# Layer 1 of a four-layer transformer kernel: feature maps of the attention moved to VectorE, its column of ones kept, one scaling moved ahead, separate PSUM banks for the last experts of layer 0, two TensorE fillers

## Chip, core and metric

The kernel runs on one core of a Trainium2 chip. The metric is the device time of one execution in microseconds (us). The engines named below are TensorE (PE, with its weight loads as PEld), VectorE (DVE), ScalarE (ACT), GpSimd (POOL) and SyncE (SP), which issues DMAs.

## What is computed

Four layers act on a residual x of 8 x 512 tokens of width 128, all in float32. Each layer is x = x + attention(layernorm(x)), then x = x + ffn(layernorm(x)). Layer 0 ends with a mixture of 16 small experts per head. The change lies mainly in the attention of layer 1, a linear attention with 16 heads of width 8:

```
def _feature_map(t): return jax.nn.elu(t) + 1.0
q, k, v = split(x @ w_qkv.T);  q, k = _feature_map(q), _feature_map(k)
kv = einsum('bhnd,bhne->bhde', k, v)
out = einsum('bhnd,bhde->bhne', q, kv) / (einsum('bhnd,bhd->bhn', q, k.sum(axis=2))[..., None] + 1e-06)
return out @ w_out.T
```

The feature map is elu(t) + 1, which is exp(t) for t below 0 and t + 1 above. It can be written min(exp(t), 1) + max(t, 0), and also exp(min(t, 0)) + max(t, 0). The FFN of layer 1 is a gated product over all tokens (called z in the code), and for 256 chosen tokens a choice of one of 8 experts. Layers 2 and 3 follow, with the experts of layer 2 and the linear layers of layer 3.

## The kernel before

The tokens are handled in eight blocks b of 512, each as J = 4 tiles of 128. Every engine executes its instructions in the order in which the program issues them: the order is written by hand, and so a step that waits holds up all that is behind it on its engine.

**Layer 0, the experts** (from L659). The units are (b, e), eight blocks by sixteen experts. `first_half` (L549) makes four products into PSUM and applies Gelu on ScalarE into `hm`; of its four results one goes to the bank `p1` and three to one of two triple banks, `threes[e % 2]`. `second_half` (L566) multiplies `hm` by the second weights into one bank from `bank()`, VectorE multiplies by the gate (L575), and POOL adds to `acc` (L581); for the very last unit the product is kept apart and not added. The loop at L681 issues the first half of unit n and the second half of unit n - 2, so for the last two turns (n = 128 and 129) only second halves are left. In this stage the pool has a single bank "one" (L533), and `bank()` (L185) gives that one unless `banks["own"]` is set. In the middle of a turn `side("P", n)` may take one step of side work on PE. `finish` (L583) multiplies the accumulated block by the output weights and adds to the residual (L270).

**Layer 1, the loop.** The tuple `stages` (L1179) lists the steps of one turn, each with a lag; at L1219 the turn i issues each step f for block i + lag. The steps that matter here:
- `turn_` (L753): four PE transposes of the normalised block `xn`, then a ScalarE copy to `xt` (L750).
- `scale`: four ScalarE instructions (L726) that make `xn` of the next block. Tiles 0 to 2 are issued after `turn_`, tile 3 as the last step of the turn.
- `project_q` (L819): q = weights x `xt` into one bank, then `exponential` (L811): Exp (L814) and Relu (L815), both from PSUM into SBUF. `q_map` (L824): POOL takes min(exp, 1) (L827) and adds relu (L828).
- `project_kv` (L830): eight products into a pair of banks, `exponential` of the keys, then a ScalarE copy of the values to `v` (L837), a tile of 129 columns. `k_map` (L839): VectorE makes the keys from exp and relu (L842), and POOL sets the 129th column of `v` to one (L843), which gives the sum of the keys.
- `gather` (L845): products of k and v on PE, then three VectorE steps to `kv`. `attend` (L861): products of q and `kv`, then VectorE divides. `turn_o` (L884): transposes and a ScalarE copy to `ot` (L889). `output` (L891): the output product and VectorE's addition to the residual (L270).
- the FFN steps `f_stats`, `f_scale`, `f_turn`, `f_gate`, `z_stats`, `z_scale`, `z_turn`, `z_out`, with lags of -3 to -7, so that only the last turns have all of them.

PSUM has two pairs "two" and four single banks "one" here (L2136), given out in turn.

**After the loop** (L1224 on) the rest is issued by hand. The normalised rows of the chosen tokens are written to DRAM by `f_scale` (DMAs at L905) and fetched by two indirect DMAs in `chosen_rows` (L999). `chosen_products` (L1006) transposes the rows and makes the gate and expert products; `chosen_gates`, `chosen_select` (L1069, L1070 on VectorE, L1073 on POOL) and others follow. At the end the first block is normalised for layer 2, POOL scatters the chosen outputs (L1169) and makes the last additions (L988, L1301), and the first queries of layer 2 follow on PE (`queries`, L1450), which need `qb`, a VectorE instruction (L2103).

`keep_clock(n)` (L777) issues n products of the identity with itself into a bank that nobody reads. It exists and is called in layers 0 and 3.

Of the kernel before, what the change touches and what calls it, by code (L numbers as in the profile page):

```python
# [160 lines left out]
def body(ctx, tc, dram, spans, x_in, ib, it, ic, ei, out):  # L161
# [114 lines left out]
    def layer0():  # L276
# [7 lines left out]
        with ExitStack() as st:  # L284
# [351 lines left out]
            with tc.manual_schedule():  # L636
# [32 lines left out]
                def first(n):  # L669
                    if n < len(units):  # L670
                        hms[n] = first_half(*units[n])
# [8 lines left out]

                for n in range(len(units) + 2):  # L681
                    first(n)

                    banks["own"] = threes[(n + 1) % 2][:, 0, :]
                    b, e = units[min(n, len(units) - 1)]
                    if e == 4 and b > 0:
                        finish(b - 1)
                    else:
                        side("P", n)
                    banks.pop("own")  # L690
                    second(n)
# [48 lines left out]
    def scale(b, part=(0, J)):  # L740
        if part[0] == 0:
            t[b]["xn"] = norm.tile([P, J, D], F32, tag="xn", name="xn")
        scaled(t[b]["xn"], x[b], t[b]["by"], part[1], part[0])
# [50 lines left out]
    def layer1():  # L794
# [9 lines left out]
        with tc.tile_pool(name="l1", bufs=2) as wp, tc.tile_pool(name="l1c", bufs=1) as once:  # L804
# [3 lines left out]
            top_row = once.tile([P, P], F32, tag="top_row", name="top_row")  # L808
            ebs = once.tile([P, 2, TB], F32, tag="ebs", name="ebs")

            def exponential(tag, src, shape):  # L811
                ex = wp.tile(shape, F32, tag=f"ex{tag}", name="ex")
                re = wp.tile(shape, F32, tag=f"re{tag}", name="re")
                nc.scalar.activation(ex, src, AF.Exp)  # L814
                nc.scalar.activation(re, src, AF.Relu)  # L815
                return ex, re


            def project_q(b):  # L819
                pq = bank()  # L820
# [1 line left out]
                t[b]["eq"] = exponential("q", pq, [P, TB])  # L822

            def q_map(b):  # L824
                ex, re = t[b]["eq"]
                t[b]["q"] = wp.tile([P, TB], F32, tag="q", name="q")
                nc.gpsimd.tensor_scalar(ex, ex, 1.0, None, ALU.min)  # L827
                nc.gpsimd.tensor_tensor(t[b]["q"], ex, re, ALU.add)  # L828

            def project_kv(b):  # L830
                pk = bank2()
                pkv = pk.rearrange("p a (j n) -> p (a j) n", j=2)
                for j in range(J):
                    mm(pkv[:, j, :], cols(t[b]["xt"], j), l1["wqkv"][:, P:])
                t[b]["ek"] = exponential("k", pkv[:, :, :P], [P, J, P])
                t[b]["v"] = v = wp.tile([P, J, P + 1], F32, tag="v", name="v")
                nc.scalar.copy(v[:, :, :P], pkv[:, :, P:])  # L837

            def k_map(b):  # L839
                ex, re = t[b]["ek"]  # L840
                t[b]["k"] = wp.tile([P, J, P], F32, tag="k", name="k")
                nc.vector.scalar_tensor_tensor(t[b]["k"], ex, 1.0, re, ALU.min, ALU.add)  # L842
                nc.gpsimd.memset(t[b]["v"][:, :, P : P + 1], 1.0)  # L843

            def gather(b):  # L845
                ps = bank()
# [329 lines left out]
            def chosen_put():  # L1176
# [14 lines left out]
                (z_turn, -7),  # L1191
                (output, -2),
                (k_map, 0),
                (f_gate, -6),
                (turn_o, -1),
                (z_out, -7),
                (f_turn, -3),
                (z_stats, -6),
                (lambda b: scale(b, (3, J)), 1),
            )  # L1200
            with tc.manual_schedule():

                nc.scalar.activation(
                    stat.tile([P, J], F32, tag="nb", name="nb")[:, :1], half[:, :1], AF.Exp
                )
                for zt in zts:
                    nc.gpsimd.memset(zt[64:65, :], 1.0)
                nc.gpsimd.memset(top_row, 0.0)
# [41 lines left out]
                z_turn(2)  # L1250
                f_gate(4)
                z_stats(4)
                chosen_products()
                chosen_gates()
                z_scale(3)
# [34 lines left out]
                by = stats_of(x[0], J)  # L1290
                z_turn(6)
                z_scale_by_vector(7)
                z_out(5)
                z_turn(7, True)
                xn = norm.tile([P, J, D], F32, tag="xn", name="xn")
# [873 lines left out]
```

## Time and profile before

| what | us |
|---|---|
| median of 3 runs | 1468.98 (1465.3 to 1469.53) |
| profiled execution, time | 1466.0 |
| profiled execution, span | 1464.2 |
| PE busy | 1387.7 (95%) |
| ACT, DVE, POOL busy | 1042.7, 982.4, 647.3 |
| layer 1 in the trace | about 396 to 523 |

The span is what the trace covers; the time of that execution is 1.8 us more. All positions below are microseconds from the start of the span. A group line gives line, engine, operation, tiles, shapes and count, then total busy time and the mean of one in ns, then the idle time of the engine ahead of it and what ended it. A timeline line gives start and length, both in us. PEclk is the granted clock of TensorE, 1.00 being full.

### The profile page before, as it was taken

To read this page: it belongs to the slowest core of one execution; us is meant where nothing else is said; L and a number is where in the kernel's file an instruction comes from. 1 tells how busy PE (TensorE), PEld (TensorE's weight loads), DVE (VectorE), ACT (ScalarE), POOL (GpSimd) and SP (SyncE) were. 2 spreads that over 40 slices of the span, in tenths; PEclk is the share of its full clock that TensorE was granted. 3 is DMA by queue.
4 is the path that set the end of the run, shared out by engine and by line. 5 is a ranking of instruction groups with operands and counts; after the bars stand their busy time and mean duration, and the time that the engine had idled before them with its cause. 6 is when DMAs were issued, how large, how long until landed. Compare 5 with 4: busy or idle time off the path is not lost.

```text
span 1464.2 us, 22177 instructions
## 1 busy us (share of the span) xinstructions
PE 1387.7 (95%) x7708; PEld 665.4 (45%) x7708; DVE 982.4 (67%) x2061; ACT 1042.7 (71%) x2131; POOL 647.3 (44%) x746
## 2 busy tenths in 40 slices
PE   7789999999889899999999999999999999999996
PEld 3652222222267554444443444455454454554465
DVE  6776655676367667633672586786787777877876
ACT  6869999999867556664865486876876767768632
POOL 6646666665655433211620172442532623524423
PEclk9999999999999999999999999999999999999999
DMA  5039999998340010101000000000000000000000
GB/s 172 1 47 133 133 132 127 131 130 123 90 150 23 26 42 22 37 1 29 1 1 1 1 1 8 1 1 8 1 1 8 1 8 1 1 8 1 1 8 15
DMA packets 33232, 59.42 MB, mean 41 GB/s; under 512 B 5601, under 2 KB 25633, under 8 KB 28642
## 3 DMA queue, kind: packets, MB, share of 16 engines
q1 hardware_dynamic: 32416, 56.18, 22.1%
q10 hardware_dynamic: 578, 1.57, 0.3%
q8 instruction: 61, 1.00, 0.3%
q14 instruction: 49, 0.40, 0.1%
q0 software_dynamic: 128, 0.26, 0.1%
HBM read 49.70 MB, written 8.29 MB: 40 GB/s over the span
## 4 chain that ended last, share of the span: by engine, by line
PE 68%; ACT 13%; DVE 9%; DMA 6%; issue 2%; POOL 1%; SPq 0%; POOLq 0%; DVEq 0%; ACTq 0%
PE ps L246 66%; DMA gs<-gates 5%; ACT hm L563 5%; ACT ex L1486 2%; ACT hm L562 2%; DVE nm L1480 1%; DVE s L715 1%; DMA gates<-eq 1%; ACT xn L1402 1%; PE ps L1816 1%; DVE x L270 1%; ACT xn L726 1%; POOL rs L243 0%; ACT h L384 0%; SPq L543 0%
## 5 line engine op out<-in xcount | busy, mean ns | idle before, releaser
L1486 ACT ACTIVATE ex<-ps,nm 128x512 f32<-128x512 f32 x512 | 346.1, 688 | 182.7 <-DVE nm L1480 178.3
L1480 DVE TENSOR_REDUCE nm<-ps 128x2 f32<-128x1024 f32 x256 | 300.4, 1215 | 60.9 <-PE ps L246 60.3
L246 PE MATMUL ps<-q,k 64*128 64x512 f32 x1024 | 256.7, 617 | 5.6 <-ACT ex L1486 4.7
L246 PE MATMUL ps<-ex,vs 128*64 128x512 f32 x1024 | 233.8, 598 | 0.0
L581 POOL TENSOR_TENSOR acc<-acc,pr 128x512 f32<-128x512 f32 x119 | 166.5, 1399 | 108.2 <-DVE pr L575 100.8
L1501 POOL TENSOR_TENSOR vs<-v,sm 128x256 f32<-128x256 f32 x128 | 81.4, 636 | 295.0 <-DVE sm L1500 267.7
L563 ACT ACTIVATE hm<-ps,blob_f 128x1536 f32<-128x1536 f32 x128 | 196.3, 1534 | 0.0
L246 PE MATMUL ps<-xt,blob_a 128*128 128x512 f32 x304 | 152.4, 628 | 0.0
L575 DVE SCALAR_TENSOR_TENSOR pr<-ps,blob_f,gs 128x512 f32<-128x512 f32 x120 | 90.0, 750 | 90.1 <-PE ps L246 73.3
L246 PE MATMUL ps<-h,w 32*128 32x512 f32 x1024 | 148.0, 639 | 2.3 <-ACT xt L750 0.8
L246 PEld LDWEIGHTS ps<-q,k 64*128 64x128 f32 x1024 | 87.1, 185 | 136.7 <-issue 69.9
L246 PE MATMUL ps<-hm,w 128*32 128x512 f32 x1024 | 136.4, 605 | 4.3 <-DVE pr L575 3.8
L246 PEld LDWEIGHTS ps<-ex,vs 128*64 128x64 f32 x1024 | 67.8, 136 | 148.5 <-issue 130.8
L1688 POOL TENSOR_TENSOR acs<-acs,prod 128x512 f32<-128x512 f32 x98 | 124.7, 1273 | 11.0 <-ACT prod L1687 6.6
L242 POOL TENSOR_SCALAR rs<-mv 128x4 f32<-128x4 f32 (+1 forms) x69 | 18.0, 261 | 198.2 <-DVE mv L1392 140.7
L1486 ACT ACTIVATION_READ_ACCUMULATOR ex<-ps,nm 128x1 f32 x512 | 104.9, 205 | 0.0
L562 ACT ACTIVATE hm<-ps,blob_f 128x512 f32<-128x512 f32 x128 | 88.1, 688 | 17.9 <-PE ps L246 17.7
L246 PEld LDWEIGHTS ps<-xt,blob_a 128*128 128x128 f32 x304 | 53.2, 194 | 87.6 <-issue 61.2
L246 PEld LDWEIGHTS ps<-h,w 32*128 32x128 f32 x1024 | 40.9, 183 | 110.3 <-ACT hm L562 92.8
L1448 DVE TENSOR_TENSOR v<-ps,blob_bc 128x512 f32<-128x512 f32 x64 | 44.2, 691 | 67.5 <-PE ps L246 43.0
L246 PEld LDWEIGHTS ps<-blob_a,ct 128*128 128x128 f32 x512 | 67.0, 191 | 32.3 <-issue 29.2
L243 POOL TENSOR_TENSOR rs<-rs,half 128x4 f32<-128x4 f32 (+1 forms) x69 | 72.5, 1051 | 5.8
(303 smaller groups left out, 2183.9 us busy)
## 6 DMA issues: line engine op xcount, KB each, us to landing
gs<-gates SPq DMA_DIRECT2D x256, 128.0 KB
blob_f<-in_f SPq DMA_DIRECT2D x1, 2560.0 KB
blob_a<-in_a SPq DMA_DIRECT2D x1, 2056.0 KB
x<-in_x SPq DMA_DIRECT2D x8, 256.0 KB
gates<-eq SPq DMA_DIRECT2D x8, 256.0 KB
ge<-gates SPq DMA_DIRECT2D x4, 512.0 KB
back<-nought SPq DMA_DIRECT2D x7, 256.0 KB
by_rows<-fxn SPq DMA_DIRECT2D x7, 256.0 KB
```

The lines of the kernel that those rows point to most:

```text
L242: nc.gpsimd.tensor_scalar(t, var, EPS, None, ALU.add)
L243: nc.gpsimd.tensor_tensor(t, t, half[:, : t.shape[-1]], ALU.pow)
L246: nc.tensor.matmul(out_, lhs, rhs, start=start, stop=stop)
L562: nc.scalar.activation(hm[:, 0, :], p1, AF.Gelu, bias=bias)
L563: nc.scalar.activation(hm[:, 1:, :], p3, AF.Gelu, bias=bias)
L575: nc.vector.scalar_tensor_tensor(pr, po, f0["b2"][:, e : e + 1], gs, ALU.add, ALU.mult)
L581: nc.gpsimd.tensor_tensor(acc[:, b, :], acc[:, b, :], pr, ALU.add)
L1448: nc.vector.tensor_tensor(v, pv, bias, ALU.add)
L1480: nc.vector.tensor_reduce(nm, ps, AX.X, ALU.max, negate=True)
L1486: nc.scalar.activation(ex[kt][:, i, :], ps[:, i, :], AF.Exp, bias=nm[:, i : i + 1], accum_out=sm[:, kt, i : i + 1],)
L1501: nc.gpsimd.tensor_tensor(vs[:, tiles, :, :], vs_[n][:, tiles, :].rearrange("p j (i n) -> p j i n", i=2), sm[:, tiles, :].unsqueeze(3).to_ ...
L1688: nc.gpsimd.tensor_tensor(t["acs"], t["acs"], p, ALU.add)
```

## The change

- In layer 0, for the last two turns of the loop, the second half writes to the second and the third bank of `threes[0]`, and the step of side work is left out of these turns.
- `exponential` computes relu(-t) from PSUM, then exp of its negative in place, which is exp(min(t, 0)); it hands on the PSUM source beside it.
- Both maps are one VectorE instruction, max(t, 0) + that, with t read from PSUM. POOL's two instructions of the query map are gone.
- `v` is one of two lasting tiles, whose columns of ones are set once, ahead of the loop; the POOL instruction in `k_map` is gone.
- Tile 3 of the next block's scaling is issued right after `k_map`, ahead of `f_gate`, `turn_o` and what follows.
- `keep_clock(9)` is put ahead of `chosen_products`, and `keep_clock(6)` ahead of `z_out(5)`.

```diff
                 for n in range(len(units) + 2):
                     first(n)
+                    if n >= len(units):
+
+                        banks["own"] = threes[0][:, 1 + n - len(units), :]
+                        second(n)
+                        banks.pop("own")
+                        continue
...
+            vts = [once.tile([P, J, P + 1], F32, tag=f"v{i}", name="v") for i in range(2)]
...
             def exponential(tag, src, shape):
                 ex = wp.tile(shape, F32, tag=f"ex{tag}", name="ex")
-                re = wp.tile(shape, F32, tag=f"re{tag}", name="re")
-                nc.scalar.activation(ex, src, AF.Exp)
-                nc.scalar.activation(re, src, AF.Relu)
-                return ex, re
+                nc.scalar.activation(ex, src, AF.Relu, scale=-1.0)
+                nc.scalar.activation(ex, ex, AF.Exp, scale=-1.0)
+                return src, ex
+
+            def feature_map(dst, src, ex):
+                nc.vector.scalar_tensor_tensor(dst, src, 0.0, ex, ALU.max, ALU.add)
...
             def q_map(b):
-                ex, re = t[b]["eq"]
                 t[b]["q"] = wp.tile([P, TB], F32, tag="q", name="q")
-                nc.gpsimd.tensor_scalar(ex, ex, 1.0, None, ALU.min)
-                nc.gpsimd.tensor_tensor(t[b]["q"], ex, re, ALU.add)
+                feature_map(t[b]["q"], *t[b]["eq"])
...
-                t[b]["v"] = v = wp.tile([P, J, P + 1], F32, tag="v", name="v")
+                t[b]["v"] = v = vts[b % 2]
...
             def k_map(b):
-                ex, re = t[b]["ek"]
                 t[b]["k"] = wp.tile([P, J, P], F32, tag="k", name="k")
-                nc.vector.scalar_tensor_tensor(t[b]["k"], ex, 1.0, re, ALU.min, ALU.add)
-                nc.gpsimd.memset(t[b]["v"][:, :, P : P + 1], 1.0)
+                feature_map(t[b]["k"], *t[b]["ek"])
...
                 (k_map, 0),
+                (lambda b: scale(b, (3, J)), 1),
                 (f_gate, -6),
                 (turn_o, -1),
                 (z_out, -7),
                 (f_turn, -3),
                 (z_stats, -6),
-                (lambda b: scale(b, (3, J)), 1),
...
+                for v in vts:
+                    nc.gpsimd.memset(v[:, :, P : P + 1], 1.0)
...
                 z_stats(4)
+                keep_clock(9)
                 chosen_products()
...
                 z_scale_by_vector(7)
+                keep_clock(6)
                 z_out(5)
```

## The prediction

> **What bounds the kernel now.** I read the page first, then busy time by stretches, then groups, waits and timeline of layer 1. On the page, the chain that ended last:
>
> ```profile
> PE 68%; ACT 13%; DVE 9%; DMA 6%; issue 2%; POOL 1%; SPq 0%; POOLq 0%; DVEq 0%; ACTq 0%
> ```
>
> TensorE (PE) carries the whole, but two thirds of it is the last two layers, from 533 us on, which the change leaves alone: they only start earlier or later. All edits lie between 388 and 526 us. That stretch in pieces of 8 us (busy PE, PEld, DVE, ACT, POOL; granted clock; DMA):
>
> ```profile
> 400.00:408.00 8.00, 5.00 (x16) 3.73 (x17) 2.06 (x13) 2.89 (x7) 3.79 (x6) 0.67 0.99 423
> 424.00:432.00 8.00, 6.96 (x46) 5.70 (x45) 6.63 (x27) 7.20 (x16) 5.13 (x10) 1.00 0.12 33
> 488.00:496.00 8.00, 7.00 (x15) 3.85 (x16) 2.93 (x16) 1.16 (x3) 1.99 (x5) 0.57 0.00 0
> 520.00:528.00 8.00, 7.22 (x24) 4.42 (x25) 3.39 (x12) 1.27 (x2) 3.46 (x3) 0.65 0.43 146
> ```
>
> Three stretches run at a low clock. In stretches of 0.1 us it reads 0.50 over 402.7-409.5, 488.0-494.9 and 518.8-525.6: 6.8 us each, after PE was thinly used. In between (second row) PE, ACT and DVE are all near 7 of 8 us. What waits in the loop of layer 1, 396 to 466 us (total, times, longest):
>
> ```profile
> PE ps L748 <- ACT xn L726: 7.1, 6, 1.8
> PE ps L246 <- POOL v L843: 2.6, 1, 2.6
> DVE x L270 <- PE ps L246: 8.7, 7, 2.2
> ```
>
> PE waits for the last tile's normalisation in six of the blocks; once, it waits for the ones column behind POOL's query map. The groups between 388 and 533 us (busy, mean ns):
>
> ```profile
> L827 POOL TENSOR_SCALAR ex<-ex 128x512 f32<-128x512 f32 x8 | 12.0, 1502 | 1.0 <-ACT ex L814 0.4
> L828 POOL TENSOR_TENSOR q<-ex,re 128x512 f32<-128x512 f32 x8 | 10.1, 1268 | 0.7
> L842 DVE SCALAR_TENSOR_TENSOR k<-ex,re 128x512 f32<-128x512 f32 x8 | 9.7, 1214 | 3.4 <-ACT re L815 3.4
> ```
>
> The timeline, at the end of layer 0 and in the loop:
>
> ```profile
> 389.52 1.06 PE L246 MATMUL ps<-hm,w 128*32 128x512 f32 x8 [0.94 <-DVE pr L575]
> 391.62 1.06 PE L246 MATMUL ps<-hm,w 128*32 128x512 f32 x8 [1.03 <-DVE pr L575]
> 428.25 1.78 DVE L842 SCALAR_TENSOR_TENSOR k<-ex,re 128x512 f32<-128x512 f32 x1
> 429.74 0.33 PE L748 MATMUL ps<-blob_c,xn 128*128 128x128 f32 x1 [0.93 <-ACT xn L726]
> ```
>
> The key map takes 0.68 us alone and 1.6-1.8 when POOL's L828 (here from 428.21) runs beside it.
>
> **Own banks for the last experts.** Each of the last two second halves waits for the VectorE read of the one shared bank (0.94, 1.03). With own banks the first starts behind 125's (388.6), the second when hm is done (389.8). VectorE's products end at 390.4 and 391.7, POOL's last addition (1.28 each from 389.6) at 392.2; then finish(7) starts, not at 393.7. POOL is late next. **-1.4 us.** The skipped side step costs nothing: its work follows in the loop after it.
>
> **Start of layer 1.** POOL held gather(0) until 403.33: rstd to 400.3, q map 1.50 + 1.26, memset 0.1. All that leaves its queue; the two lasting memsets (0.1 each) run before the others. From finish at 392.2 the chain is: finish 1.85, project_q 1.0, project_kv 1.9 (ends 397.0), Relu 0.5, Exp 0.6, copy of v 0.5 (398.6), key map 0.75. gather(0) at 399.45: 3.9 earlier, so **-2.5** beside the 1.4.
>
> **The maps.** Two ACTIVATEs stay two, but Exp now reads what Relu writes. Independent ones start 0.50 apart (L814, L815: 0.60 and 0.59 long), so about +0.13 each, 0.26 a block. VectorE gains a query map, with no row of its own: below, 0.68 (the SBUF form alone), above 1.78 (that form beside POOL); I take 0.75, of L575, the same operation from PSUM. It is queued ahead of the residual addition L270 and the key map. L270 waits there for PE's output product, 1.02 us in most blocks, so 0.75 is hidden; uncovered it would be 0.75 x 8 = 6.0. The key map goes from 1.7 to 0.75. VectorE's sum per block is thus about 0.2 lower and POOL's 2.9.
>
> A rule speaks against the last: the Trainium skill ("PSUM — Partial Sum Buffer", PSUM bank collisions raise a hardware error) says that two engines must not touch one bank at once, reads included. The key map would then follow the copy of v, 0.5 us later than Exp's end. The row agrees: in layer 0 VectorE's L364 starts at 30.84, when ScalarE's first copy of the same bank (30.23) is over. I take 0.5 more: keys are ready 2.65 us after project_kv instead of 1.95. The PSUM slots are held longer (query bank to its map, the pair to the key map); their next users come four and two allocations later, after these ends: nothing.
>
> **Last tile's scaling ahead.** Before: after project_kv ScalarE does two ACTIVATEs, v, o, f (0.5 each), then the tile (0.4); PE's last transpose waits and ScalarE waits 0.42 for it, before xt (0.6). After: the tile comes before o and f, and the 0.42 is filled. From project_kv's end to xt 0.04+0.6+0.6+0.5+0.4+0.5+0.5+0.6 = 3.7; then project_q, attend, project_kv 4.2-4.3. Period 8.0 with FFN stages, 7.5 without; before 8.14, 8.28, 8.4, 8.5, 9.64, 9.91 (between gathers). The six: -0.6, -0.3, -0.4, -0.5, -0.6, -0.3 = **-2.7**. The first period, 10.4 at the low clock, falls to 9.8 (**-0.6**), or to 7.5 if the clock holds (2.3 more).
>
> **The fillers.** A 128x128 matmul is two instructions; eight take 1.06 (0.11 each). Nine: 2.0 us; PE is idle from 485.27 to 487.30, waiting for gathered rows, so they cost 0 there, 2.0 if PE comes late. Six: 1.35 into the 1.38 idle before z_out(5) (515.77-517.15): 0. What they buy: at 488.0-494.9 PE works 5.4 us at half clock, so 2.7; VectorE's gates (491.3-494.0) follow, then its two steps per half (0.69 each); POOL's second product L1073 moves from 498.73 to about 496.3: **-2.4**. At 518.8-525.6 PE would be done 3.0 earlier, but the first query waits for qb, and VectorE's qb for POOL's chain (L1169, L988, L1301, to 524.27), which no filler moves. Query at 524.5 instead of 526.05: **-1.4**; POOL is late next.
>
> Here the skill and the rows part. "TensorE: Matmul & The Clock Gate" (Why this matters for your kernels) puts the drop at PE-idle gaps above about 3 us. By it, the third stretch had no reason (longest idle 1.38 us), the sixfold filler would buy nothing, and the new start (2.5 us between products, with three transposes inside) would stay at full clock: -2.3 there, +1.4 here. The trace: drops lie on a grid of 3.41 us (402.69, 488.00, 518.76); the windows before them had 0.3, 1.0 and 2.0 us of busy PE, or 0, 0.7, 1.2 without transposes; one with 1.5 of products (409.5-412.9) did not drop. By the rows under about 1.4 us of products drops the clock. So the start still drops when the window covers 2.05 of its 2.5 us: (0.94 + 0.9)/3.41, about half of the phases; the ninefold filler leaves 2.15 us between products and fails in about 4 of 10. I follow the rows.
>
> **Sum** against the profiled execution (1466.0, span 1464.2): 1.4 + 2.5 + 0.6 + 2.7 + 2.4 + 1.4 = 11.0; the start's 2.3 (half) and the lost 2.4 (4 in 10) about cancel. 1466.0 - 11.0 = 1455.0. The median of the runs, 1469.0, lies 3.0 above the profiled one, and no row says why; I add a third: **1456**.
>
> **Rivals.**
> - Forecast, 1451-1460: 0.6.
> - Half of it: the loop keeps its period because ScalarE is full (7.2 of 8, plus the 0.26), and the clock drops at the ninefold filler. For: ScalarE's share. Then 1.4 + 2.5 + 0.6 + 1.4 = 5.9, or 1460-1463 by profile or median: 0.24.
> - Nothing: what the start gains is given back at the gathered rows, where a DMA of 3.15 us and two gathers wait. Against: their inputs come from the same chain. 1465-1472: 0.09.
> - Slower: VectorE becomes the loop's bound. The query map (0.75), the wait for v (0.5) and the slower Exp (0.26) all lie on the path: 1.5 x 8 = 12.1; only 1.4 + 2.5 are saved, +8.2, so 1474. It decides where L270's idle before it is below 0.75; it is 1.02. 0.07.
>
> 0.3% (4.4 us) is about what a measurement can tell from no change: under 1464.6 is faster, above 1473.4 slower. Faster 0.85, same 0.09, slower 0.06. The range, 1450 to 1464, takes in the held start and the half case.
>
> **What would show it.** After: no L827/L828 group on POOL; the key map near 0.75 with no long forms; no wait of PE on POOL for v; the wait of L748 on xn under 2 us in all; periods of about 8 between gathers; finish of layer 0 1.4 earlier; clock 1.00 at the chosen products and the first queries. I am wrong if L270 waits for the query map, if the fillers end after the rows have landed, or if a low clock shows at new places.

## The result, and the profile after

| | before | after |
|---|---|---|
| median of 6 runs, us | 1466.7 (1463.92 to 1469.53) | 1452.85 (1450.44 to 1456.5) |
| profiled execution, time | 1466.0 | 1450.44 |
| its span | 1464.2 | 1448.7 |

The ratio is 0.9906, 95% interval 0.9887 to 0.9925: 13.9 us faster, 3 us more than the 11.0 of the sum. The median was put at 1456 (1451 to 1460) and is 1452.85. Measured once more, against runs of the kernel before on the same chip, the changed kernel gave 0.9928 (0.9915 to 0.9941), which is 10.7 us. The profiled execution after is the fastest of its six, so the two traces differ by 15.5 us in span, more than the medians do. Those 15.5 us are the ones that can be placed.

The chain that ended last, on the page of the changed kernel, is the same as before but for 1% at SP's queue: the last layers carry it.

```profile
PE 68%; ACT 13%; DVE 9%; DMA 6%; issue 2%; POOL 1%; SPq 1%; POOLq 0%; DVEq 0%; ACTq 0%
```

The changed stretch of the changed kernel in pieces of 8 us (columns as before: length, busy PE, PEld, DVE, ACT, POOL, then the granted clock and the DMA share):

```profile
400.00:408.00 8.00, 6.45 (x38) 4.91 (x37) 4.80 (x20) 5.92 (x13) 1.46 (x3) 1.00 0.97 373
416.00:424.00 8.00, 7.78 (x51) 6.55 (x51) 7.05 (x32) 7.71 (x17) 3.53 (x7) 1.00 0.11 33
480.00:488.00 8.00, 7.13 (x41) 5.03 (x40) 7.43 (x27) 5.00 (x14) 3.35 (x3) 1.00 0.00 0
504.00:512.00 8.00, 5.79 (x33) 3.76 (x33) 5.37 (x15) 2.70 (x6) 4.48 (x4) 1.00 0.25 86
```

All four stand at clock 1.00, also those at 400, at the chosen products and at the first queries, which stood at 0.67, 0.57 and 0.65. In the loop (second row) PE is busy 7.78 of 8 us where it had 6.96, and ScalarE 7.71 where it had 7.20. POOL has 3.53 left of 5.13: the query map went to VectorE, whose share rose only from 6.63 to 7.05.

The groups of the two maps, between 386 and 520 us (busy, mean ns, then idle time ahead), and the waits of the loop between 396 and 466 us (total, times, longest), both of the changed kernel:

```profile
L828 DVE SCALAR_TENSOR_TENSOR k<-ps,ex 128x512 f32<-128x512 f32 x8 | 5.5, 692 | 4.0 <-ACT v L846 4.0
L828 DVE SCALAR_TENSOR_TENSOR q<-ps,ex 128x512 f32<-128x512 f32 x8 | 5.5, 682 | 0.3 <-ACT ex L824 0.3
```

```profile
DVE k L828 <- ACT v L846: 4.0, 8, 1.4
PE ps L754 <- ACT xn L732: 3.9, 3, 1.9
DVE x L270 <- PE ps L246: 3.2, 7, 0.9
PE ps L246 <- DVE k L828: 0.2, 1, 0.2
```

A map costs 0.69 us, with no long form among the eight (the longest is 0.69). The wait of PE on POOL for the ones column is gone, and that on `xn` has shrunk from 7.1 to 3.9 us, of which 1.9 and 1.5 stand in the first two blocks. The key map waits all eight times for the copy of `v`. That is a new wait, but PE then waits for the key map just once, 0.2 us.

**Where the 15.5 us went.** I cut both traces at the same events; "gather(i)" is the first product of a gather, a fetched row counts when PE starts to transpose it (L1017), "the first query" is the start of ScalarE's first instruction of layer 2's queries (L1469), which needs PE's product and `qb`, and each row is the time from the event before it.

| from, to | before | after | difference | predicted |
|---|---|---|---|---|
| up to layer 0's last Gelu (L563) | 388.26 | 387.77 | -0.5 | none |
| Gelu to finish(7) | 5.45 | 4.02 | -1.4 | -1.4 |
| finish(7) to gather(0) | 9.62 | 7.38 | -2.2 | -2.5 |
| gather(0) to gather(1) | 10.42 | 7.46 | -3.0 | -0.6, or -2.9 if the clock holds |
| gather(1) to gather(7) | 52.81 | 49.47 | -3.3 | -2.7 |
| gather(7) to second fetched row on PE | 21.98 | 20.87 | -1.1 | none |
| to POOL's second product of the gates | 10.19 | 7.52 | -2.7 | -2.4 |
| to the first query | 27.32 | 25.94 | -1.4 | -1.4 |

They sum to -15.6; behind the first query the rest takes as long as before to 0.1.

The end of layer 0 and the loop, in the timeline of the changed kernel:

```profile
390.01 1.06 PE L246 MATMUL ps<-hm,w 128*32 128x512 f32 x8 [1.06 <-DVE pr L575]
391.79 0.49 PE L246 MATMUL ps<-blob_f,acc 128*128 128x128 f32 x2 [0.71 <-POOL acc L581]
...
413.33 0.69 DVE L828 SCALAR_TENSOR_TENSOR k<-ps,ex 128x512 f32<-128x512 f32 x1 [0.19 <-ACT v L846]
413.74 0.33 PE L754 MATMUL ps<-blob_c,xn 128*128 128x128 f32 x1 [0.56 <-ACT xn L732]
...
419.86 0.69 DVE L270 TENSOR_TENSOR x<-x,ps 128x512 f32<-128x512 f32 x1 [0.42 <-PE ps L246]
```

The first of the two last expert halves no longer waits. The second, at 390.01, still waits 1.06 us for a VectorE product, although it has a bank of its own and Gelu was done at 389.30. Finish starts behind POOL's last addition, 0.71 after PE ran dry. In the loop L270 still waits 0.42 us for PE: the query map, which ends at 419.44, has used up part of the former 1.02 and no more. The former wait, in the timeline of the kernel before:

```profile
427.65 0.69 DVE L270 TENSOR_TENSOR x<-x,ps 128x512 f32<-128x512 f32 x1 [1.02 <-PE ps L246]
```

The loop's 3.3 us are not spread evenly. The periods from gather(1) on were 8.14, 8.28, 8.28, 8.56, 9.64, 9.91 and are 7.45, 7.49, 7.50, 7.50, 8.65, 10.88: four give 3.3 together, the fifth 1.0, and the last loses that 1.0 again. The timeline of the changed kernel behind gather(6), at 445.22:

```profile
446.43 0.87 DVE L721 BATCH_NORM_STATS2 s<-x 128x6 f32<-128x128 f32 x4
...
448.44 1.25 PE L246 MATMUL ps<-kv,q 128*128 128x144 f32 x8 [1.16 <-DVE kv L866]
```

PE comes to attend with nothing else to do and waits 1.16 us for `kv`, where it waited 0.27 before. The products of gather(6) end at 446.35, but VectorE's queue has two sets of statistics (of `z` and of `x`) ahead of the three steps to `kv`, which start at 447.77. In the fifth period PE is busy for all of its 8.65 us. So here, and here alone in the loop, VectorE is late next. This exchange between the last two periods comes with the moved tile: the kernel with that move alone, below, has 8.70 and 10.83 us and waits 1.12 us for `kv`.

### The profile page after: what moved, and what is told of

Same layout as the page of the kernel before. It is cut to its first block, busy times and chain, and to the rows that moved or that the text cites. A ratio compares the mean times of both kernels' runs of the same rounds, so it can differ in the third digit from the quotient of the medians.

```text
span 1448.7 us, 22220 instructions
## 1 busy us (share of the span) xinstructions
PE 1382.2 (95%) x7738; PEld 663.2 (46%) x7738; DVE 984.8 (68%) x2069; ACT 1044.2 (72%) x2131; POOL 623.7 (43%) x724
## 3 DMA queue, kind: packets, MB, share of 16 engines
q8 instruction: 62, 1.02, 0.3%
## 4 chain that ended last, share of the span: by engine, by line
PE 68%; ACT 13%; DVE 9%; DMA 6%; issue 2%; POOL 1%; SPq 1%; POOLq 0%; DVEq 0%; ACTq 0%
PE ps L246 66%; DMA gs<-gates 5%; ACT hm L563 4%; ACT ex L1497 2%; ACT hm L562 2%; DMA gates<-eq 1%; DVE nm L1491 1%; DVE s L721 1%; ACT xn L1413 1%; SPq L543 1%; ACT xn L732 1%; PE ps L1827 1%; ACT h L384 0%; DVE pr L575 0%; POOL rs L243 0%
## 5 line engine op out<-in xcount | busy, mean ns | idle before, releaser
L563 ACT ACTIVATE hm<-ps,blob_f 128x1536 f32<-128x1536 f32 x128 | 196.4, 1535 | 0.0
L1699 POOL TENSOR_TENSOR acs<-acs,prod 128x512 f32<-128x512 f32 x98 | 124.6, 1271 | 10.7 <-ACT prod L1698 6.3
```

What stands on the lines that cost most here:

```text
L563: nc.scalar.activation(hm[:, 1:, :], p3, AF.Gelu, bias=bias)
L1699: nc.gpsimd.tensor_tensor(t["acs"], t["acs"], p, ALU.add)
```

## The experiments

My theory was that the gain has three parts: a shorter chain at the start, a loop that loses the wait on the last tile, and clock drops avoided at three places. The rivals were that the loop gains through one part only, that VectorE is now its bound, and that the fillers do nothing. Each kernel is timed against the kernel before on its own chip, so the ratios are what compares. The milestones of all traces, in us, are in one table (columns: Gelu to finish(7), finish to gather(0), gather(0) to (1), (1) to (7), second row to gates, gates to first query, and the whole from Gelu to first query); an asterisk marks an interval into which a low clock fell in that trace.

| kernel | ratio, 95% interval | Gelu-fin. | -g(0) | -g(1) | -g(7) | row-gates | -query | whole |
|---|---|---|---|---|---|---|---|---|
| before | | 5.45 | 9.62* | 10.42* | 52.81 | 10.19* | 27.32* | 137.79 |
| after | 0.9906 (0.9887-0.9925) | 4.02 | 7.38 | 7.46 | 49.47 | 7.52 | 25.94 | 122.66 |
| after_again | 0.9928 (0.9915-0.9941) | 4.01 | 9.01* | 9.02* | 49.44 | 7.51 | 25.93 | 126.59 |
| only_own | 0.9980 (0.9970-0.9991) | 4.02 | 11.28* | 10.30* | 52.77 | 10.05* | 27.33* | 137.94 |
| only_maps | 0.9967 (0.9953-0.9982) | 6.21* | 9.33* | 7.69 | 52.95* | 9.21* | 27.33* | 133.72 |
| only_scale | 0.9993 (0.9985-1.0002) | 5.45 | 9.62* | 9.26* | 52.78 | 10.09* | 27.34* | 136.52 |
| only_fill | 0.9989 (0.9977-1.0001) | 5.45 | 9.62* | 9.78* | 52.77 | 9.21* | 27.56* | 136.33 |
| no_fill | 0.9921 (0.9904-0.9937) | 4.02 | 7.38 | 7.47 | 49.46 | 9.21* | 27.34* | 126.30 |
| query_twice | 0.9914 (0.9897-0.9930) | 4.02 | 7.39 | 9.01* | 49.45 | 9.21* | 27.59* | 128.59 |
| pool_query | 0.9886 (0.9869-0.9902) | 4.02 | 7.38 | 7.91 | 49.76 | 7.46 | 25.94 | 123.07 |
| pool_query_again | 0.9908 (0.9894-0.9923) | 4.02 | 7.38 | 7.92 | 49.76 | 7.46 | 25.94 | 123.08 |
| more_fill | 0.9905 (0.9888-0.9922) | 4.02 | 9.68* | 7.39 | 49.46 | 7.52 | 26.54 | 125.52 |
| fill_all | 0.9906 (0.9892-0.9921) | 6.02 | 7.28 | 7.46 | 49.45 | 7.52 | 26.56 | 124.93 |
| fill_all_pool | 0.9910 (0.9896-0.9924) | 6.01 | 7.29 | 7.91 | 49.76 | 7.52 | 26.40 | 125.84 |

### One part alone

**only_own.** The kernel before, with the own banks of the last experts and nothing else:

```diff
+                    if n >= len(units):
+                        banks["own"] = threes[0][:, 1 + n - len(units), :]
+                        second(n)
+                        banks.pop("own")
+                        continue
```

> The kernel before with the own banks for the last two experts alone. My theory: from the start of ScalarE's last Gelu (L563) to the first product of finish(7) 5.45 us before, 4.0 now, because POOL's addition is late next and not the one shared bank; all else as before, so the time falls by 1.4 us, 0.1%, too little for the timed runs and to be read from the trace. Rival: the two side steps that are left out come back in the loop after finish and take the gain away: then finish starts 1.4 earlier, but the first query product of layer 1 does not.

Timed, 0.998: about -2.9 us (-4.4 to -1.3). In the trace Gelu to finish(7) takes 4.02 as in the changed kernel, so the -1.4 belongs to this part alone. But finish to gather(0) takes 11.28 us instead of 9.62. The timeline of this kernel shows why:

```profile
392.07 0.63 PE L246 MATMUL ps<-blob_f,pr 128*128 128x128 f32 x2
```

A pair of finish's products takes 0.63 where the changed kernel's trace has 0.39: the clock is low from 391.7 to 395.1. In this one execution a drop gave back what the part had gained; the timed runs say that it doesn't always. The rival, that the two side steps take the time back after finish, would show in every kernel with own banks; the changed kernel has 7.38 us from finish to gather(0).

**only_maps.** The edits of `exponential`, both maps and the lasting `v` tiles alone, tile 3 staying where it was:

```diff
-                nc.gpsimd.tensor_scalar(ex, ex, 1.0, None, ALU.min)
-                nc.gpsimd.tensor_tensor(t[b]["q"], ex, re, ALU.add)
+                feature_map(t[b]["q"], *t[b]["eq"])
...
-                nc.vector.scalar_tensor_tensor(t[b]["k"], ex, 1.0, re, ALU.min, ALU.add)
-                nc.gpsimd.memset(t[b]["v"][:, :, P : P + 1], 1.0)
+                feature_map(t[b]["k"], *t[b]["ek"])
```

> The kernel before with the maps on VectorE from PSUM and the lasting ones columns, without the moved scaling, own banks and fillers. My theory: from finish(7) to gather(0) 9.6 us before, 7.4 now (POOL's queue is out of the way). From gather(1) to gather(7) 52.8 us before, here 52.0 to 52.8, almost nothing: PE's last transpose still waits for the last tile, which comes as late as before. Long key maps (1.6 to 1.8 us) are gone, all near 0.69. Time: -2.2, and 2.3 more if the clock holds at the start. Rival: the maps by themselves are what shortens the loop (VectorE freed of the long key map): gather(1) to gather(7) 50 or 51 us.

**only_scale.** Only the move of tile 3:

```diff
                 (k_map, 0),
+                (lambda b: scale(b, (3, J)), 1),
...
-                (lambda b: scale(b, (3, J)), 1),
```

> The kernel before with the last tile's scaling moved ahead, and nothing else. My theory: it needs the maps. PE's last transpose no longer waits, but the gather behind it then waits for the key map, which is still 1.6 to 1.8 us long: gather(1) to gather(7) 52.8 us before, 51.9 to 52.6 here; finish(7) to gather(0) unchanged at 9.6. Time within 1 us. Rival: the two parts add up, and this one carries most of the loop's 3.3 us: 50.0 to 50.5 us.

Timed, the maps bring about -4.8 us (-6.9 to -2.6) and the move -1.0 (-2.2 to +0.3). In the loop, from gather(1) to gather(7), the move alone brings nothing: 52.78 against 52.81. The maps alone seem to bring nothing either (52.95), but a low clock, from 411.0 to 414.4, fell into the first of their six periods (columns as in the tables of pieces above):

```profile
410.22:419.40 9.18, 8.13 (x43) 6.60 (x43) 5.70 (x22) 5.55 (x11) 1.46 (x3) 0.81 0.87 256
419.40:427.51 8.11, 7.01 (x48) 5.92 (x47) 7.03 (x34) 7.57 (x16) 2.93 (x6) 1.00 0.11 32
```

The other five, at full clock, are 8.11, 8.11, 8.11, 9.57 and 9.87, together 0.9 us less than before. So the maps alone are worth about 0.9 us in the loop, a little more if the first period gained too, the move nothing, and both together 3.3. Two timelines tell why. With the maps alone:

```profile
425.96 0.69 DVE L822 SCALAR_TENSOR_TENSOR k<-ps,ex 128x512 f32<-128x512 f32 x1 [0.19 <-ACT v L840]
...
427.35 0.33 PE L748 MATMUL ps<-blob_c,xn 128*128 128x128 f32 x1 [1.10 <-ACT xn L726]
```

With the move alone:

```profile
426.28 1.77 DVE L842 SCALAR_TENSOR_TENSOR k<-ex,re 128x512 f32<-128x512 f32 x1
...
428.20 1.13 PE L246 MATMUL ps<-v,k 128*128 128x129 f32 x8 [1.09 <-DVE k L842]
```

With the maps alone the keys are ready at 426.65, but PE comes to the gather only behind the last transpose of the turn, which waits 1.10 for `xn` until 427.35. With the move alone that transpose isn't late any more, and the gather behind it waits 1.09 us for the long key map, which ends at 428.05. The period has two late arrivals of nearly one length; taking one away hands most of its time to the other. So most of the loop's 3.3 us, some 2.4, belong to the pair. The largest gain of the maps in their own trace is at the first blocks: gather(0) to gather(1) takes 7.69 instead of 10.42, where POOL no longer holds gather(0) and the clock held.

**only_fill and no_fill.** The two fillers added to the kernel before, and the changed kernel without them (the same two lines taken out):

```diff
+                keep_clock(9)
                 chosen_products()
...
+                keep_clock(6)
                 z_out(5)
```

> The kernel before with the two fillers alone. My theory: no low clock at the chosen products and at the first queries, where the kernel before had it; POOL's second product L1073 2.4 us earlier against the gathered rows, the first query of layer 2 another 1.4: -3.8 in all where the kernel before has both low stretches, and about -3 on the average of runs. The low stretch at the start of layer 1 stays. Rival[...]: the smaller filler buys nothing, -2.4. Other rival: fillers are work on PE, +3.4 us if they end after what they cover.

> The changed kernel without its two fillers. My theory: the clock is at half for 6.8 us at the chosen products (PE idle above 4 us in any phase of the 3.41 us windows) and, in about half of the executions, at the first queries: +2.4 and +1.4 x 0.5, so 3.1 us slower than the changed kernel, 0.2%. Rival: the changed order leaves PE busier before these places, so the fillers buy nothing: 0.

only_fill measured 0.9989, about -1.6 us (-3.4 to +0.1), half of the 3 us that I expected on the average of runs. no_fill measured 0.9921 (0.9904 to 0.9937), between the two values of the changed kernel, 0.9906 and 0.9928. Against the one the fillers are worth 2 us, against the other they cost 1, and the intervals are wider than that: there they can't be told from nothing. In the traces they gain where the clock holds: no_fill has 9.21 and 27.34 where the changed kernel has 7.52 and 25.94, 3.1 us in all. How much the first is worth depends on the drop that it avoids: a low stretch of 3.4 us at the chosen products makes row to gates 9.21 long (no_fill, only_maps), one of 6.8 us 10.1 to 10.2 (before, only_own, only_scale). What fails is holding the clock. In only_fill it dropped at both places behind the fillers (490.3 to 493.7 and 521.0 to 524.4). The timeline of only_fill at the two places:

```profile
484.58 2.17 PE L246 MATMUL ps<-blob_c 128*128 128x128 f32 x18
488.76 0.61 PE L246 MATMUL ps<-blob_l,xm 128*128 128x9 f32 x4 [0.46 <-ACT xm L1011]
...
514.08 1.50 PE L246 MATMUL ps<-blob_c 128*128 128x128 f32 x12
...
521.14 3.57 PE L246 MATMUL ps<-xt,blob_a 128*128 128x512 f32 x4 [1.27 <-issue]
```

Between the end of the ninefold filler (486.75) and the next product (488.76) lie 2.0 us without products. Behind the sixfold one (to 515.58) come three stretches of products (to 519.88), then transposes and 1.27 us of idle time ahead of the first queries, which no filler covers: these four products then take 3.57 us, against 1.96 in the changed kernel's trace. Over all traces the chosen products ran at a low clock in 5 of 5 without the ninefold filler and in 2 of 6 with it and no other there; the first queries' products in 5 of 5 without the sixfold one and in 2 of 7 with it alone. In a third of these seven, more_fill, the clock dropped just behind the first query (514.9 to 518.4), and what follows took 1.7 us longer.

### Is VectorE the loop's bound?

**query_twice.** The changed kernel with the query map computed twice (the second writes the same values again):

```diff
                 feature_map(t[b]["q"], *t[b]["eq"])
+                feature_map(t[b]["q"], *t[b]["eq"])
```

> The changed kernel with the query map done twice in each block (the second one writes the same values): 0.69 us more on VectorE ahead of the residual addition and the key map, eight times. My theory: VectorE is not the loop's bound; its idle of 0.42 ahead of the residual addition and the wait of the key map for the copy of v take most of it: gather(1) to gather(7) 49.5 to 50.5 us, time +0 to +1. Rival (the slower case of the prediction): VectorE is on the path, and each costs in full: +0.69 x 6 = 4.1 us in the loop, 5.5 in all.

**pool_query, pool_query_again.** The changed kernel with the query map back on POOL, Exp and Relu both from PSUM as before:

```diff
-                t[b]["eq"] = exponential("q", pq, [P, TB])
...
+                nc.scalar.activation(ex, pq, AF.Exp)
+                nc.scalar.activation(re, pq, AF.Relu)
+                t[b]["eq"] = ex, re
...
-                feature_map(t[b]["q"], *t[b]["eq"])
+                ex, re = t[b]["eq"]
+                nc.gpsimd.tensor_scalar(ex, ex, 1.0, None, ALU.min)
+                nc.gpsimd.tensor_tensor(t[b]["q"], ex, re, ALU.add)
```

> The changed kernel, but the query map is POOL's two instructions again (with Exp and Relu from PSUM); the key map stays on VectorE from PSUM. It tells why the key map became short. My theory[...]: a key map with one operand in PSUM doesn't contend, so it takes 0.69 us beside POOL's L828 too, and the loop loses little: gather(1) to gather(7) 49.5 us in the changed kernel, up to 50.5 here. The time rises by 0 to 1 us. Rival: POOL's absence is what made it short: key maps of 1.6 to 1.8 us come back and the loop is 52 us or more.

> The changed kernel with the query map on POOL again, with more runs. In its first trace the way from gather(0) to gather(7) took 57.7 us against 56.9 in the changed kernel, and yet its few runs were 2 to 3 us shorter. My theory: those runs had no low clock by chance; with more runs it is 0 to 1 us slower than the changed kernel. Rival: POOL's query map is the better place, and it is 2 us faster again.

The doubled map costs the loop nothing: gather(1) to gather(7) takes 49.45 against 49.47. The timeline of query_twice shows where the 0.7 us goes:

```profile
430.13 1.41 DVE L828 SCALAR_TENSOR_TENSOR q<-ps,ex 128x512 f32<-128x512 f32 x2
431.45 0.68 DVE L270 TENSOR_TENSOR x<-x,ps 128x512 f32<-128x512 f32 x1
```

L270 has no idle time ahead of it now: the second map has used up its 0.42 us, and the rest is taken where the key map would have waited for `v`; it starts at 432.10. So the slower rival falls, and not narrowly. The 5.9 us that this trace has over that of the changed kernel all lie outside the loop: 1.6 at gather(0) to (1), 1.7 and 1.7 at the two fillers, each with a drop of the clock, and 1.1 between gather(7) and the fetched rows. The timed ratio, 0.9914, lies between the two of the changed kernel.

pool_query moves the map back and loses 0.3 us in the loop and 0.45 in the first period. Its timeline, in one block:

```profile
411.95 1.27 POOL L843 TENSOR_TENSOR q<-ex,re 128x512 f32<-128x512 f32 x1
412.41 0.69 DVE L828 SCALAR_TENSOR_TENSOR k<-ps,ex 128x512 f32<-128x512 f32 x1 [0.18 <-ACT v L852]
```

The key map takes 0.69 with POOL's addition beside it from start to end. In the kernel before it took 1.6 to 1.8 in the four blocks in which the two overlapped, reading two tiles in SBUF. So the PSUM operand made it short, and not POOL's absence. The query map on VectorE is thus worth well under a microsecond in the trace; the loop gains by the key map from PSUM together with tile 3. The lasting ones columns were not tried alone.

Yet pool_query was timed at 0.9886, the lowest of all (the changed kernel itself was not timed on that chip). Neither of its traces has a low clock anywhere between 380 and 520 us, and its eight runs lie between 1449.6 and 1452.9, those of the changed kernel (twelve) between 1450.4 and 1458.1. Timed beside the changed kernel on one chip, it was 0.9908 against 0.9928, about 3 us less, though 0 to 1 more was expected. That put the question whether it is better or just drops less often, for which the last kernels were made.

### Filling every gap

**more_fill.** The changed kernel with two further fillers, ahead of the second block's transposes and behind the copy of the fetched rows:

```diff
+                        if (f, i) == (turn_, 1):
+                            keep_clock(14)
...
                 nc.scalar.copy(xm, ps[:, :256])
+                keep_clock(3)
```

> The changed kernel with two fillers more: fourteen products ahead of the transposes of block 1 (PE waits there 1.9 us for the last tile), and three between the transposes of the gathered rows and the chosen products (0.46 us of idle). My theory: in about half of the executions of the changed kernel the clock drops at the start of layer 1 (2.3 us), and in 4 of 10 at the chosen products (2.4 us); this one never drops there. So 0 to 5 us faster, 2 on the average, with less spread, and the same as the best executions of the changed kernel, 1450. Rival: the changed kernel already keeps its clock there, and the fillers cost up to 0.5 us.

I had mis-sized this one: each product is two instructions, so the filler at the second block took 3.3 us. The clock dropped before it all the same, from 392.1 to 395.5, in finish. The first period with the filler was 7.39, the row to gates 7.52, both at full clock. The ratio, 0.9905, is that of the changed kernel: no gain of 2 us.

**fill_all, fill_all_pool.** Fillers in all gaps that had shown a drop: four and three products ahead of the last two expert halves (into the first bank of `threes[0]`), seven ahead of the second block's transposes, two behind the copy of the fetched rows, five behind `z_out(7)`. fill_all_pool has the query map of pool_query besides.

```diff
                         banks["own"] = threes[0][:, 1 + n - len(units), :]
                         second(n)
+                        banks["own"] = threes[0][:, 0, :]
+                        keep_clock(4 if n == len(units) else 3)
...
+                keep_clock(2)
...
+                            keep_clock(7)
...
+                keep_clock(5)
```

> The changed kernel with fillers in all the gaps where a trace showed a drop, sized to the idle time there (0.22 us a product): four and three after the last two experts (1.07 and 0.72 us idle), seven ahead of the transposes of block 1 (1.9), two after those of the gathered rows (0.46), five after the last z_out (1.27). The fourteen of the kernel with more fillers were twice too many: 28 instructions of 0.11 are 3.1 us, not 1.55. My theory: no low clock between 380 and 520 us in any execution, so 1450 to 1451, 2 us less than the changed kernel. Rival: what the fillers save in clock they cost in order, and the time is the same; or low stretches still come.

> The same fillers, and the query map on POOL. If the clock explains the short times of the kernel with POOL's query map, this is 0 to 1 us slower than the kernel with all fillers and VectorE's query map; if POOL is the better place, 2 us faster than that.

> The changed kernel once more, on one chip with the three others of this call, as their base. From the drops of the clock seen so far (a stretch of 3.4 or 6.8 us at half clock, in some executions, at the end of layer 0, the start of layer 1, the chosen products and the first queries) I expect 1452.5, spread over 5 us.

No low clock shows between 385 and 520 us in either trace, and the spread of the runs is small (fill_all 1451.3 to 1453.2). The median of fill_all, 1452.59, misses the expected 1450 to 1451. It is 2.4 us under that of after_again on the same chip, but the intervals of the two ratios overlap, and 0.9906 is also what the changed kernel had the first time. In the trace, a part of what the held clock saves is lost again, at two places. The first is the end of layer 0, in the timeline of fill_all:

```profile
390.50 1.16 PE L246 MATMUL ps<-blob_c 128*128 128x128 f32 x8 [0.97 <-DVE pr L575]
```

The filler doesn't fill the wait of the second half (1.06 us in the changed kernel): it waits itself, 0.97 us, for the same VectorE product, and the half comes behind its four products, 1.0 us later. The other three wait 0.94 us for VectorE's last product and take 0.8 us ahead of finish(7), which comes 2.0 us later in all. The banks of both halves and of the fillers belong to one tile, `threes[0]`, whose other banks VectorE's products read; that PE waits for the tile and not for the bank fits these waits and that of the second half in the changed kernel, but no run put the filler into another tile.

The second place is the way to the first query, 26.56 us against 25.94. The five products behind `z_out(7)` are not the cause: more_fill, which doesn't have them, takes 26.54. Its timeline there:

```profile
512.46 0.73 DVE L2117 TENSOR_SCALAR qb<-blob_a 128x8 f32<-128x8 f32 x1 [1.89 <-POOL x L995]
513.27 0.69 ACT L1472 ACTIVATE q<-ps,qb 128x512 f32<-128x512 f32 x1 [4.56 <-DVE qb L2117]
```

The query waits for `qb` behind POOL, and POOL for its first scatter of the chosen outputs (L1176 of the changed kernel), which takes 3.1 to 3.3 us to land in more_fill, fill_all and fill_all_pool, and 2.4 in the other eleven traces. Why is open. In fill_all PE's products for the query are done at 512.24, 1.0 us before the query starts. Without the 2.0 and the 0.6 us fill_all would stand at about 122.3 from Gelu to query, the same as the changed kernel's lucky trace. fill_all_pool takes 0.9 us more than fill_all in the trace and 0.3 more in the timed median: with the clock held in both, POOL's query map isn't better. after_again is the changed kernel itself, at 1455.0 where I expected 1452.5: its trace has 126.59 against 122.66, and the 3.9 us nearly all lie in the two intervals with a drop (3.2; from 390.4 to 393.8 and from 400.6 to 404.1) and at the fetched rows (0.8). Its loop and its last two columns agree with the first trace to 0.03.

Why pool_query's two traces and eight runs escaped the drops stays open. Its start is 0.4 us longer, which shifts what follows against the grid on which drops lie; that this is the cause was not shown, and chance isn't excluded either.

## Why the prediction was right, step by step

**Right, with its size.** The own banks (-1.4 said, -1.43 measured, POOL next as written, and only_own has the same 4.02). One step of it was not as written: the second half was to start when `hm` is done, and starts 0.71 us after Gelu's end, behind VectorE; it costs nothing, because finish waits for POOL's last addition (to 391.74) and reads the late product (ready at 391.95) only at 392.11. The start (-2.5, -2.24). The gates, where the clock holds (-2.4, -2.67). L270's idle time hides the query map: 0.42 of it are left. The key map follows the copy of `v`, every time. The page "PSUM — Partial Sum Buffer" of the Trainium skill (PSUM bank collisions raise a hardware error) agrees here with 4.0 us of such waits, eight times. The keys are ready 2.49 us after project_kv; the prediction's 2.65 is a slip, its own terms give 2.45.

**The first query: right in size by luck.** -1.4 was said and -1.38 measured, but by another wait than the one named. The query was to wait for `qb` behind POOL, with PE done 3.0 us earlier. In the changed kernel it waits for PE:

```profile
510.43 0.69 ACT L1469 ACTIVATE q<-ps,qb 128x512 f32<-128x512 f32 x1 [3.96 <-PE ps L246]
```

PE's products end at 510.39, `qb` is ready at 510.06. The products start as long behind the gates as before (23.95 us, before 23.99), after 1.27 us of idle time, and take 1.96 us instead of 3.29; that is the 1.4. VectorE's addition L796 ends 0.10 us before they start, and in more_fill a wait of 0.36 us at this place is put down to it. That `qb` would have allowed nearly the same time is chance.

**The first period** could go two ways, and I gave the held clock half of the phases. The changed kernel's first trace held it; of seven traces with the new start (after, after_again, no_fill, query_twice, more_fill, both pool_query) four held it from finish to gather(1) and three did not.

**The loop: mechanism right, size short.** -2.7 said, -3.3 measured. Two terms were off, in opposite ways. The first is "project_q, attend, project_kv 4.2-4.3" in the period of 8.0. The four periods became 7.5, which gives 3.3 for them and not 1.8 (0.6, 0.3, 0.4, 0.5; the third and the fourth were 8.28 and 8.56 before, not 8.4 and 8.5). From project_kv's end to the end of the copy to `xt` it takes 3.61 us, 3.7 said; from there to the next project_kv's end 3.89, where it took 4.31 before. The copy to `xt` and the project_q behind it, before and after:

```profile
430.10 0.59 ACT L750 COPY xt<-ps 128x512 f32<-128x512 f32 x1 [0.42 <-PE ps L748]
431.14 1.02 PE L246 MATMUL ps<-xt,blob_l 128*128 128x512 f32 x2
```

```profile
429.44 0.60 ACT L756 COPY xt<-ps 128x512 f32<-128x512 f32 x1
430.09 1.12 PE L246 MATMUL ps<-xt,blob_l 128*128 128x512 f32 x2
```

Before, PE was still in the gather when `xt` was done (430.69) and began project_q 0.45 us later. With earlier keys the gather is all but over by then, and project_q follows `xt` (430.04) at once. With the move alone, where the gather waits for the keys, it begins 1.00 us behind `xt` (428.17 and 429.17). This is the share of the shorter key map, to which the prediction gave none: it put the whole on the move of tile 3, and the move alone brings nothing. In a period of 7.50 us PE is now busy for 7.28 and ScalarE for 7.37. The second term is the last two periods, put at -0.9 together; they give nothing. PE is then fully busy in one, and waits for VectorE's statistics in the other, which my list of what is late next didn't have.

**One sign missed.** The wait of the transposes on `xn` was to fall under 2 us and is 3.9. But 3.3 of it lie ahead of gather(0) and gather(1), and in the loop 0.56 are left.

**The fillers: mechanism right, size too big for a mean.** The sum has 3.8 us for them, less an offset for 4 in 10 failures. In the profiled pair the two places give 4.0, of which about 1.0 is there because the kernel before happened to have the longer drop. Over many runs the fillers gave -1.6 alone, and nothing that can be told on top of the other parts. The step "the first queries at full clock" was put down to the sixfold filler without a chance of failing; it failed in 2 of 7 traces, and what lies behind it, transposes and 1.27 us of idle time, is the likely reason, though only the two kernels with five more products there speak for it (no drop in two traces). Where a filler failed, row to gates took 9.21, as in no_fill and only_maps without it, and gates to first query 27.56 and 27.59 where 27.33 was had without it.

**The clock by rule and by row.** The rule of the Trainium skill's page "TensorE: Matmul & The Clock Gate" (Why this matters for your kernels), gaps above about 3 us, would have had no drop at the first queries; 5 of 5 traces without the filler had one, with 1.38 us as the longest idle before it in the kernel before. So the rows decided rightly against it. But the rule that the prediction drew from four windows, a drop below about 1.4 us of products without transposes, fails too. Two windows of the kernel before, the one ahead of the third drop and one of the loop:

```profile
515.30:518.72 3.42, 2.04 (x18) 1.73 (x17) 2.34 (x15) 3.18 (x9) 2.05 (x4) 1.00 0.00 0
443.63:447.04 3.41, 2.38 (x21) 1.98 (x19) 2.55 (x4) 2.99 (x7) 2.65 (x3) 1.00 0.27 77
```

The second has 0.85 us of products without transposes, fewer than the first with 1.3, and no drop followed. Counted over all fourteen traces between 380 and 530 us, in windows laid on each trace's grid, a drop followed 18 of the 45 windows with less than 1.4 us of products, and 8 windows with more. With the transposes in the sum the split is cleaner: below 1.6 us of busy PE a drop followed each of 12 windows, between 1.6 and 2.2 us 14 of 46, above 2.2 us none of 533. What decides in between is open. New drops came at the end of layer 0 in four traces (only_own, only_maps, more_fill, after_again), a place that I hadn't named, though "if a low clock shows at new places" was among the ways to be wrong.

**What was not predicted.** 1.1 us between gather(7) and the second fetched row. The changed kernel's own two traces have 20.87 and 21.67 us there, so most of it may be chance; but the four traces without the new maps have 21.9 to 22.2 and the ten with them 20.6 to 21.9, so a part may belong to the maps. Which part is not shown. The half microsecond before the last Gelu lies ahead of every edit; over the traces that Gelu starts anywhere from 386.3 to 390.1. And a third of 3.0 added for the median wasn't needed: before's median over more runs is 1466 to 1467, close to the profiled 1466.0.

**The rivals.** "Half" and "nothing" fall by the loop (49.47 against 52.81) and by the ratio's interval. "Slower" falls by query_twice.

## What to carry to other kernels

When two arrivals at an engine lie within a few tenths of each other, cost an edit that takes away one of them at little and the pair at the full time, and test it by making each alone; before reading such a test, see whether the clock held in both traces. Judge a clock filler by many runs and by the busy products in the whole stretch that follows, not by one trace in which the clock held: here one trace said 4 us and the runs of the whole kernel could not tell it from nothing. See that a filler doesn't itself wait for what it is to bridge: here one with a bank of its own in a tile that VectorE still read stood behind the wait and lengthened it.

## What the runs showed of the hardware

- A VectorE scalar_tensor_tensor over 128x512 takes 0.69 us with one operand in PSUM, alone or beside POOL's addition; with both in SBUF it took 0.68 or 0.69 alone (four blocks) and 1.6 to 1.8 beside it (four blocks).
- Between 380 and 530 us low stretches of the clock (0.50) last 3.41 or 6.83 us and begin on a grid of 3.41 us within a run (in the kernel before at 402.67, 488.00 and 518.72: 25 and 9 steps). One and the same kernel met them at other places in two traces, 3.9 us apart in this stretch.
- No drop followed a window of that grid with more than 2.2 us of busy PE (533 windows), and one followed each of the 12 with less than 1.6.
- An ACTIVATE that reads what the one before it wrote starts 0.63 us behind it (416.13 and 416.76 in the changed kernel), two independent ones 0.50: 0.13 each, as estimated.
- A 128x128 product in fp32 is two instructions of 0.11 us at full clock (the ninefold filler of only_fill: 18 in 2.17 us, with the last one's end).
